# Attention and tree layers on one core: scores and the next maxima back to back on eight shared PSUM banks, and the product with v once per group

## The chip, the cores and the metric

The kernel runs on one core of a Trainium2 chip. The time is the device time of one execution in microseconds, over 3 runs. Its core has TensorE (PE; PEld are its weight loads), VectorE (DVE), ScalarE (ACT), GpSimd (POOL) and SyncE (SP, which issues all DMAs here).

## The reference

Eight sequences of 512 tokens with 256 features pass through four residual layers. All is float32.

```python
x = x + attn_a(layernorm(x))    # 16 heads of 16, biases, softmax over all 512 keys
x = x + ffn(layernorm(x))       # below
x = x + attn_b(layernorm(x))    # 16 heads of 16, rotary q and k, causal softmax
x = x + ffn(layernorm(x))       # the same ffn, the same weights

def ffn(x):
    gate = sigmoid((x @ Wq.T) @ routers.T)       # 255 nodes of a binary tree, depth 8
    leaf_prob = product over the 8 levels of (1 - gate) or gate     # 256 leaves
    return (leaf_prob @ leaf_values) @ Wout.T + Wout_b
```

An attention layer computes `softmax(q k^T / 4) v` for each of the 16 heads, and then a product with an output matrix.

## The kernel before

**Sequences, groups, steps.** The program handles 16 "sequences" n: n = 0 to 7 are the eight batch rows in the first attention and tree layer (non-causal), n = 8 to 15 the same rows in the second (causal). A sequence has four groups g of four heads (NG = NJ = 4), and a group has four tiles of 128 keys, kt. One group and one kt make a step: 16 steps a sequence, 256 in all.

**Scores.** q and k are split into a high and a low part and laid out so that one head takes 32 partitions. Four heads then use four row groups of TensorE at a time, as 32*128 matmuls (`passes`, L416). `scores` computes transposed scores st[keys, queries] for one kt into four PSUM banks: two matmuls per head with k against the two arrangements of q, and a third (`ones` against `m`) that subtracts each query's maximum. ScalarE then writes exp of it to the SBUF tiles pt (L481). In the causal half, st has only the queries from kt * 128 on, and GpSimd clears the upper triangle of the diagonal block (L484).

**Maxima.** The row maxima are found earlier from untransposed scores mx (`maxima`, two matmuls per head, four banks). VectorE reduces each bank to one column (L444; with the mask in the causal half, L439). After four tiles of queries, VectorE makes `less` (L448, L449), TensorE transposes it (`lessT`, in `put`), ScalarE copies it to `rows` (L460), and a DMA puts it into one of two tiles m (L461). The maxima run LEAD = 12 half-steps, that is six steps, ahead of the scores.

**Product with v.** `weigh` multiplies v with pt as 128*32 matmuls (L498), one head per column group, right after the scores of the next step. It adds the four kt of a group up in a bank of its own (`ps_av`), so av has one bank and seven banks rotate among all other tiles (`bank`, pool `banks`). Every fourth kt ScalarE copies av to o4 (L504), and DMAs carry sums and outputs on to `divide`.

**Everything else** is cut into units, generators that a small planner (`Units`) advances: `pre` (LayerNorm, transposes, q, k and v of a coming sequence), `post` and `tree` (output product y, LayerNorm, gates z, the tree's levels lp on VectorE, transposes lt, leaf values ty), `divide`, `put`. Each unit names its kind ("big" and "small" for TensorE, "v" VectorE, "g" GpSimd, "row") and a delay. In each step `share` grants TensorE a budget of TENSOR = 11 and VectorE one of 3900, and `products` pulls units until TensorE's is used up. Full-width products and transposes use the whole array (128*128). The row x of each sequence stays in SBUF from its load at the start to the store at the end: eight tiles x0 to x7.

**Order.** The loop runs over half-steps i. An even i issues the maxima of the step six steps ahead and then products; an odd i issues the scores of this step, then `weigh` of the step before. `in_program_order` ties each engine's instructions to the order in which the program issued them, so an engine never overtakes, and a DMA that waits on SP holds those behind it.

Of the kernel before, what the change touches and what calls it, by code (L numbers as in the profile page):

```python
# [41 lines left out]
F32 = mybir.dt.float32  # L42
# [20 lines left out]
STEPS = NG * NT * 2  # L63
LEAD = 12

EARLY = 6


FULL, TRANSPOSE, TENSOR = 12, 4, 11
# [7 lines left out]
class Units:  # L77
# [40 lines left out]
    def share(self):  # L118
        self.tensor = min(self.tensor, TENSOR // 2) + TENSOR
        self.vector = min(self.vector, VECTOR // 2) + VECTOR  # L120
# [19 lines left out]
def hybrid_kernel(ctx, tc, x, a_qk, a_v, a_o, a_qk_b, a_v_b, a_o_b, b_q, b_k, b_v, b_o,  # L140
# [3 lines left out]
    stream = ctx.enter_context(tc.tile_pool(name="stream", bufs=1))  # L144
# [18 lines left out]
    xs = []  # L163

    def load_x(b):
        t = stream.tile([P, NT, D], F32, tag=f"x{b}", name=f"x{b}")
        nc.sync.dma_start(t, x[b].rearrange("(t p) d -> p t d", p=P))
        xs.append(t)
# [8 lines left out]
    for m in ms:  # L177
# [19 lines left out]
    pool5 = ctx.enter_context(tc.tile_pool(name="w5", bufs=5))  # L197
# [3 lines left out]
        for w, n, tag in ((f_q, "f_q", "lpT"), (f_routers, "f_routers", "th"),  # L201
                          (f_values, "f_values", "lp"), (f_out, "f_out", "out"))
    ]
    banks = ctx.enter_context(tc.tile_pool(name="banks", bufs=7, space=PSUM))
    dram = ctx.enter_context(tc.tile_pool(name="apart", bufs=2, space=bass.MemoryType.DRAM))
    ps_av = ctx.enter_context(tc.tile_pool(name="ps_av", bufs=1, space=PSUM))
# [7 lines left out]
    for b in range(3, B):  # L214
        load_x(b)
# [4 lines left out]
    vs, ks, qs, outs, avs, lesses = [], {}, {}, {}, {}, {}  # L220
# [28 lines left out]
    def fold_bias():  # L249

        vb = pool1.tile([P, NC, P], F32, tag="vb", name="vb")
        for c in range(NC):
            nc.vector.tensor_copy(vb[:, c, :], v_b[:, c : c + 1].to_broadcast([P, P]))
        ps = bank([P, D], "vbo")
        for c in range(NC):
            nc.tensor.matmul(ps, lhsT=vb[:, c, :], rhs=wa.o[:, c, :], start=c == 0, stop=c == NC - 1)
        nc.vector.tensor_tensor(out_b, ps, out_b, ALU.add)

    def layer_norm(b, name, got):

        x = xs[b]
        stats = pool2.tile([P, NT, 6], F32, tag="ln_stats", name=f"ln_stats{name}")
        mv = pool2.tile([P, NT, 2], F32, tag="ln_mv", name=f"ln_mv{name}")
        for t in range(NT):
            nc.vector.bn_stats(stats[:, t, :], x[:, t, :])
            nc.vector.bn_aggr(mv[:, t, :], stats[:, t, :])
            units.spend(vector=D + 2 * START)
            if t == 1:
                yield "v", 0
        yield "g", 1  # L270
        less_mean = pool2.tile([P, NT], F32, tag="ln_less", name=f"ln_less{name}")
        nc.gpsimd.tensor_scalar(less_mean, mv[:, :, 0], -1.0, None, ALU.mult)
        rstd = pool2.tile([P, NT], F32, tag="ln_rstd", name=f"ln_rstd{name}")
        nc.gpsimd.tensor_scalar(rstd, mv[:, :, 1], EPS, None, ALU.add)
        nc.gpsimd.tensor_tensor(rstd, rstd, neg_half, ALU.pow)
        xn = pool2.tile([P, NT, D], F32, tag="xn", name=f"xn{name}")
        for t in range(NT):
            if t % 2 == 0:
                yield "g", 0
            nc.gpsimd.tensor_scalar(  # L280
                xn[:, t, :], x[:, t, :], less_mean[:, t : t + 1], rstd[:, t : t + 1], ALU.add, ALU.mult
            )
        got.append(xn)

    def add_bias(b, bias):
        for t in range(0, NT, 2):
            yield "g", 0
            part = xs[b][:, t : t + 2, :]
            nc.gpsimd.tensor_tensor(part, part, bias.unsqueeze(1).to_broadcast([P, 2, D]), ALU.add)
# [50 lines left out]
    def pre(n):  # L340

        causal, b = divmod(n, B)
# [6 lines left out]
        w = wb if causal else wa  # L349
        got = []  # L350
        yield from layer_norm(b, f"n{n}", got)
# [14 lines left out]
        free = (n - 1) * STEPS + 2 + LEAD  # L366
        vals[n] = units.add(by_tokens(xnT, w.v, D, f"v{n}", values), "big", max(1, free - units.now), rank=4)
        for which in range(2):
# [3 lines left out]
            for c in range(NC):  # L372
                yield "big", 0 if c or which else 1
# [34 lines left out]
        if not causal:  # L408
            yield from add_bias(b, out_b)
# [8 lines left out]
    def maxima(n, g, u):  # L418

        causal = n >= B  # L420
        qt = (u + LEAD // 2) % NT
# [43 lines left out]
    def scores(n, g, kt):  # L465
# [12 lines left out]
        for pair in range(2):  # L478
            pt = pool5.tile([P, 2, S], F32, tag="pt", name=f"pt{n}_{g}_{kt}_{pair}")
# [11 lines left out]
    def weigh(n, g, kt, pts):  # L491

        if kt == 0:
            avs[n, g] = ps_av.tile([P, S], F32, tag="av", name=f"av{n}_{g}")
        av = avs[n, g]
        first = kt * P if n >= B else 0
        for j in range(NJ):
            nc.tensor.matmul(  # L498
                av[32 * j : 32 * j + 32, first:], lhsT=vs[n % 2][:, kt, g * NJ + j, :, :].rearrange("p d s -> p (d s)"),
                rhs=pts[j // 2][:, j % 2, : S - first], start=kt == 0, stop=kt == NT - 1,  # L500
            )
        if kt == NT - 1:
            o4 = pool1.tile([P, S], F32, tag="o4", name=f"o4{n}_{g}")
            nc.scalar.copy(o4, avs.pop((n, g)))  # L504
            if g == 0:
                outs[n] = (
                    pool2.tile([P, NC, S], F32, tag="out", name=f"out{n}"),
                    pool2.tile([P, NC, S // HD], F32, tag="few", name=f"few{n}"),
                )
            outT, few = outs[n]  # L510
            to, c = slice(g % 2 * 64, g % 2 * 64 + 64), g // 2
            nc.sync.dma_start(few[to, c, :], o4[1 :: 2 * HD, :])
            nc.sync.dma_start(outT[to, c, :], o4[::2, :])
            if g % 2:
                units.add(divide(n, c), "v", 3, rank=0)
# [19 lines left out]
    def to_x(b):  # L535
        def add(ps, t, count):
            part = xs[b][:, t : t + count, :]
# [5 lines left out]
    def post(n):  # L543

        causal, b = divmod(n, B)
# [3 lines left out]
        yield from by_tokens(outT, (wb if causal else wa).o, D, f"y{n}", to_x(b))  # L549
        yield "v", 1  # L550
        yield from tree(n, b)

    def tree(n, b):
# [4 lines left out]
        yield from layer_norm(b, f"t{n}", got)  # L558
# [15 lines left out]
        yield from add_bias(b, f_bias)  # L574
# [23 lines left out]
        yield from by_tokens(lpT, wl, D, f"ty{n}", to_x(b), 1)  # L598
        if n >= B:
            nc.sync.dma_start(out[b].rearrange("(t p) d -> p t d", p=P), xs[b])  # L600
# [14 lines left out]
    waiting = deque()  # L615
    for i in range(-LEAD, total + 2):
# [5 lines left out]
        for n in range(2, 2 * B):  # L622
            if ahead == (n - 1) * STEPS - (EARLY if n >= B else 0):
                if n >= B:
                    units.finish(trees[n - B])
                pres[n] = units.add(pre(n), rank=1 if n >= B else 3)
        if i % STEPS == 0 and i // STEPS in vals:
            units.finish(vals.pop(i // STEPS))
        if i % 2 == 0:
            units.share()  # L630
            if ahead < total:
                maxima(*place(ahead))
            units.products()
        else:
            if 0 <= i < total:
                waiting.append((*place(i), scores(*place(i))))
            if len(waiting) > 1 or (i >= total and waiting):
                weigh(*waiting.popleft())
            units.pull("row")
# [76 lines left out]
```

## Time and profile before

| | |
|---|---|
| median of 3 runs (lowest, highest) | 1237.98 us (1235.34, 1238.89) |
| profiled execution | 1241.78 us, its span 1240.1 us |
| busy in the span | PE 1157.4, PEld 602.2, DVE 854.0, ACT 639.0, POOL 412.2 us |
| mean granted clock of TensorE | 0.944 |
| DMA queue q1 | 81.55 MB, 18.6% of 16 engines |

The span runs from the first to the last instruction. Busy times of different engines overlap. The ends of matmuls are modelled, so that PE's busy time holds some waits too; the starts are what can be compared. The chain of waits is followed back from the last instruction to what released each step. A group's idle time is that of its engine just before it, with the instruction that ended it.

### The profile page before, as it was taken

To read this page: it belongs to the slowest core of one execution; us is meant where nothing else is said; L and a number is where in the kernel's file an instruction comes from. 1 tells how busy PE (TensorE), PEld (TensorE's weight loads), DVE (VectorE), ACT (ScalarE), POOL (GpSimd) and SP (SyncE) were. 2 spreads that over 40 slices of the span, in tenths; PEclk is the share of its full clock that TensorE was granted. 3 is DMA by queue.
4 is the path that set the end of the run, shared out by engine and by line. 5 is a ranking of instruction groups with operands and counts; after the bars stand their busy time and mean duration, and the time that the engine had idled before them with its cause. 6 is when DMAs were issued, how large, how long until landed. Compare 5 with 4: busy or idle time off the path is not lost.

```text
span 1240.1 us, 24920 instructions
## 1 busy us (share of the span) xinstructions
PE 1157.4 (93%) x8916; PEld 602.2 (49%) x8916; DVE 854.0 (69%) x2400; ACT 639.0 (52%) x1457; POOL 412.2 (33%) x636
## 2 busy tenths in 40 slices
PE   4899999999999999999999989999999999999965
PEld 2444444545445354444455555555545455555443
DVE  2766686776777578778878786867778686767422
ACT  2266566575666557655564534545353544534431
POOL 3222232230323213322244444444443445423331
PEclk9699999999999899999999999989898998988788
DMA  8031103021030301303030211213021211310110
GB/s 314 18 113 67 71 19 118 19 84 49 16 122 20 115 13 41 121 20 121 16 121 13 89 62 44 94 37 121 26 87 53 86 70 37 122 33 21 37 36 17
DMA packets 61211, 83.14 MB, mean 67 GB/s; under 512 B 14752, under 2 KB 27808, under 8 KB 61088
## 3 DMA queue, kind: packets, MB, share of 16 engines
q1 hardware_dynamic: 61088, 81.55, 18.6%
q8 instruction: 70, 1.15, 0.4%
q14 instruction: 53, 0.43, 0.1%
HBM read 16.52 MB, written 4.72 MB: 17 GB/s over the span
## 4 chain that ended last, share of the span: by engine, by line
PE 69%; DVE 16%; DMA 4%; POOL 4%; issue 4%; ACT 3%; SPq 1%; DVEq 0%; ACTq 0%; POOLq 0%
PE st L416 16%; PE av L498 13%; PE mx L416 11%; PE qk L376 7%; DVE seen L439 6%; PE ty L310 6%; PE v L310 5%; PE z L310 5%; PE y L310 3%; DVE most L444 3%; ACT pt L481 2%; DVE lp L589 2%; POOL xnt L280 2%; DMA m<-rows 1%; DMA q<-hl 1%
## 5 line engine op out<-in xcount | busy, mean ns | idle before, releaser
L481 ACT ACTIVATE pt<-st 128x512 f32<-128x512 f32 (+3 forms) x1024 | 446.8, 523 | 334.3 <-PE st L416 332.5
L444 DVE TENSOR_REDUCE most<-mx 128x1 f32<-128x512 f32 x512 | 317.2, 682 | 163.6 <-PE mx L416 163.4
L439 DVE CUSTOM_DVE_ANT_0 seen<-mx,mask 128x128 f32<-128x128 f32 (+3 forms) x512 | 250.6, 490 | 129.4 <-PE mx L416 72.5
L416 PE MATMUL st<-q,k 32*128 32x512 f32 (+3 forms) x2048 | 240.5, 426 | 22.4 <-DVE most L439 15.0
L498 PE MATMUL av<-pt,v 128*32 128x512 f32 (+3 forms) x2048 | 238.2, 537 | 3.5 <-POOL pt L484 2.3
L416 PE MATMUL mx<-k,q 32*128 32x512 f32 (+3 forms) x2048 | 210.1, 427 | 16.8 <-DMA k<-hl 5.8
L484 POOL TENSOR_SCALAR_AFFINE_SELECT pt<-pt 128x256 f32<-128x256 f32 x256 | 110.5, 440 | 318.7 <-ACT pt L481 315.8
L416 PEld LDWEIGHTS st<-q,k 32*128 32x128 f32 x2048 | 114.5, 187 | 152.6 <-issue 66.4
L416 PEld LDWEIGHTS mx<-k,q 32*128 32x128 f32 x2048 | 102.3, 192 | 169.4 <-issue 36.0
L416 PE MATMUL st<-m,ones 32*128 32x512 f32 (+3 forms) x1024 | 118.5, 365 | 1.3 <-DMA m<-rows 1.3
L322 POOL TENSOR_TENSOR hl<-r,hl 128x512 fp32r<-128x512 f32 x32 | 41.7, 1304 | 190.5 <-ACT hl L392 184.5
L310 PE MATMUL ty<-wl,lpT 128*128 128x256 f32 x256 | 80.4, 471 | 0.0
L498 PEld LDWEIGHTS av<-pt,v 128*32 128x32 f32 x2048 | 41.1, 109 | 78.7 <-issue 59.2
L416 PEld LDWEIGHTS st<-m,ones 32*128 32x128 f32 x1024 | 70.7, 190 | 9.3 <-DMA m<-rows 3.4
L589 DVE SCALAR_TENSOR_TENSOR lp<-th,lp 128x8 f32<-128x8 f32 (+6 forms) x224 | 70.2, 353 | 2.9
L310 PE MATMUL z<-wg,txnT 128*128 128x255 f32 x256 | 68.5, 408 | 0.0
L310 PEld LDWEIGHTS ty<-wl,lpT 128*128 128x128 f32 x256 | 57.4, 235 | 18.0 <-ACT pt L481 5.5
L376 PE MATMUL qk<-xnT,a_qk 128*128 128x512 f32 x128 | 63.9, 635 | 0.0
L376 PE MATMUL qk<-xnT,b_qk 128*128 128x512 f32 x128 | 62.9, 617 | 0.0
L310 PEld LDWEIGHTS z<-wg,txnT 128*128 128x128 f32 x256 | 47.7, 199 | 17.1 <-ACT pt L481 7.1
L531 POOL TENSOR_TENSOR out<-out,den 128x512 f32<-128x512 f32 x32 | 41.4, 1294 | 35.8 <-DMA den<-apart 35.6
L396 POOL TENSOR_TENSOR r<-r,r 128x512 f32<-128x512 f32 x32 | 40.3, 1278 | 24.8 <-DVE r L387 24.8
(76 smaller groups left out, 1101.4 us busy)
## 6 DMA issues: line engine op xcount, KB each, us to landing
q<-hl SPq DMA_DIRECT2D x128, 256.0 KB
k<-hl SPq DMA_DIRECT2D x64, 256.0 KB
out<-o SPq DMA_DIRECT2D x64, 128.0 KB
den<-apart SPq DMA_DIRECT2D x32, 256.0 KB
x<-x SPq DMA_DIRECT2D x8, 512.0 KB
out<-x SPq DMA_DIRECT2D x8, 512.0 KB
m<-rows SPq DMA_DIRECT2D x64, 16.0 KB
few<-o SPq DMA_DIRECT2D x64, 8.0 KB
```

The lines of the kernel that those rows point to most:

```text
L310: nc.tensor.matmul(ps[:, i, :n], lhsT=srcT[:, c, (t + i) * P : (t + i + 1) * P], rhs=w[:, c, :], start=c == 0, stop=c == NC - 1,)
L322: on.tensor_tensor(hl[:, 1, :], raw, hl[:, 0, :].bitcast(F32), ALU.subtract)
L376: nc.tensor.matmul(ps, lhsT=wt[:, k, c * P : (c + 1) * P], rhs=xnT[:, k, :], start=k == 0, stop=k == NC - 1,)
L396: nc.gpsimd.tensor_tensor(raws[c], raws[c], raws[2 + c], (ALU.subtract, ALU.add)[c])
L416: nc.tensor.matmul(ps, lhsT=lhsT, rhs=rhs, start=i == 0, stop=i == len(operands) - 1)
L439: nc.vector.tensor_tensor_reduce(out=seen[:, :width], in0=ps[:, :width], in1=mask[:, S - width :], scale=1.0, scalar=LOWEST, op0=ALU.add, ...
L444: nc.vector.tensor_reduce(at, ps, AX.X, ALU.max)
L481: nc.scalar.activation(pt[:, i, : S - first], ps[:, : S - first], AF.Exp, scale=SCALE)
L484: nc.gpsimd.affine_select(out=pt[:, :, :P], in_=pt[:, :, :P], pattern=[[0, 2], [1, P]], compare_op=ALU.is_ge, fill=0.0, base=0, channel_mu ...
L498: nc.tensor.matmul(av[32 * j : 32 * j + 32, first:], lhsT=vs[n % 2][:, kt, g * NJ + j, :, :].rearrange("p d s -> p (d s)"), rhs=pts[j // 2 ...
L531: nc.gpsimd.tensor_tensor(outT[:, c, :], outT[:, c, :], den, ALU.mult)
L589: nc.vector.scalar_tensor_tensor(pairs[:, :, :, side], of_level, one, lp, ALU.add, ALU.mult)
```

## The change

The odd and even half-steps are merged: one turn of the loop issues the scores of a step and, directly behind them, the maxima of the step six steps ahead. The bank for av is given up, and eight banks rotate among all tiles. `weigh` is called once per group, after the first step of the next group, with all four kt (16 products); for that, ten pt tiles are kept where there were five. Products follow at the end of a turn; TENSOR is 15, and a call of `weigh` costs WEIGH = 13 of it. The order of query tiles in `maxima` becomes 1, 2, 3, 0. `pre` of a coming sequence starts EARLY = 8 half-steps earlier in both halves, has rank 2, and holds its q and k products back until 24 half-steps into the sequence two back.

To make room in SBUF, only AT_ONCE = 5 tiles x exist. The tree of each sequence of the first half stores its row to DRAM (`store_x`), and `pre` of a later sequence loads what it needs (`load_x`), three half-steps before LayerNorm reads it. Three scratch tiles share the buffers of others, and the scratch ring of GpSimd's DMAs is set to 8192.

```diff
-EARLY = 6
-FULL, TRANSPOSE, TENSOR = 12, 4, 11
+AT_ONCE = 5
+EARLY = 8
+FULL, TRANSPOSE, WEIGH, TENSOR = 12, 4, 13, 15
...
-        self.tensor = min(self.tensor, TENSOR // 2) + TENSOR
+        self.tensor = min(self.tensor, TENSOR // 4) + TENSOR
...
+    def load_x(n):
+        t = stream.tile([P, NT, D], F32, tag="x", name=f"x{n}")
+        src = x[n] if n < B else between[n - B]
+        nc.sync.dma_start(t, src.rearrange("(t p) d -> p t d", p=P))
+        xs[n] = t
+
+    def store_x(n):
+        dst = between[n] if n < B else out[n - B]
+        nc.sync.dma_start(dst.rearrange("(t p) d -> p t d", p=P), xs.pop(n))
...
-    pool5 = ctx.enter_context(tc.tile_pool(name="w5", bufs=5))
+    pool10 = ctx.enter_context(tc.tile_pool(name="w10", bufs=10))
...
-    banks = ctx.enter_context(tc.tile_pool(name="banks", bufs=7, space=PSUM))
+    banks = ctx.enter_context(tc.tile_pool(name="banks", bufs=8, space=PSUM))
...
-    ps_av = ctx.enter_context(tc.tile_pool(name="ps_av", bufs=1, space=PSUM))
...
+        if n not in xs:
+            units.finish(trees[n - AT_ONCE])
+            load_x(n)
+            yield "v", 3
...
-                yield "big", 0 if c or which else 1
+                free = (n - 2) * STEPS + 24 + LEAD
+                yield "big", 0 if c or which else max(1, free - units.now)
...
-        qt = (u + LEAD // 2) % NT
+        qt = (1, 2, 3, 0)[u]
...
-    def weigh(n, g, kt, pts):
-        if kt == 0:
-            avs[n, g] = ps_av.tile([P, S], F32, tag="av", name=f"av{n}_{g}")
-        av = avs[n, g]
+    def weigh(n, g, group):
+        av = bank([P, S], f"av{n}_{g}")
+        for kt, pts in enumerate(group):
...
-        if n >= B:
-            nc.sync.dma_start(out[b].rearrange("(t p) d -> p t d", p=P), xs[b])
+        store_x(n)
...
-        if i % 2 == 0:
-            units.share()
-            if ahead < total:
-                maxima(*place(ahead))
-            units.products()
-        else:
-            if 0 <= i < total:
-                waiting.append((*place(i), scores(*place(i))))
-            if len(waiting) > 1 or (i >= total and waiting):
-                weigh(*waiting.popleft())
-            units.pull("row")
+        units.share()
+        full = group if len(group) == NT else None
+        if full:
+            group = []
+        if 0 <= i < total:
+            group.append(scores(*place(i)))
+        if ahead < total:
+            maxima(*place(ahead))
+        units.reductions()
+        units.pull("g")
+        units.tick()
+        if full:
+            weigh(*place(i - 2)[:2], full)
+            units.spend(tensor=WEIGH)
+        units.pull("row")
+        units.products()
```

## The prediction

> **What bounds the kernel now.** I read the page first, then the waits, the timeline of one step, and the windows around a stretch of low clock.
>
> ```profile
> span 1240.1 us, 24920 instructions
> PE 1157.4 (93%) x8916; PEld 602.2 (49%) x8916; DVE 854.0 (69%) x2400; ACT 639.0 (52%) x1457; POOL 412.2 (33%) x636
> ...
> PE 69%; DVE 16%; DMA 4%; POOL 4%; issue 4%; ACT 3%; SPq 1%; DVEq 0%; ACTq 0%; POOLq 0%
> ```
>
> TensorE carries 69% of the chain that ended last, VectorE 16%. Nothing else matters, so the question is what fills TensorE's 93%. One step (a kt of one group) without causal mask reads:
>
> ```profile
> 303.51 0.74 PE L416 MATMUL mx<-k,q 32*128 32x512 f32 x8
> 304.18 1.99 PE L310 MATMUL y<-a_o,out 128*128 128x256 f32 x8
> 306.10 0.74 PE L416 MATMUL st<-q,k 32*128 32x512 f32 x8
> 306.66 0.41 PE L416 MATMUL st<-m,ones 32*128 32x512 f32 x4
> 307.01 1.06 PE L498 MATMUL av<-pt,v 128*32 128x512 f32 x8
> 308.00 0.74 PE L416 MATMUL mx<-k,q 32*128 32x512 f32 x8
> 308.57 0.39 PE L416 MATMUL st<-q,k 32*128 32x512 f32 x1
> ```
>
> Take differences of starts, not durations. Inside a block the single records of the trace start one pass (four matmuls side by side in four row groups, 512 columns) every 0.216 us. So mx is worth 0.432, but takes 0.67 (303.51 to 304.18); y is worth 8 x 0.216 = 1.73 and takes 1.92; st with ones 0.648 and takes 0.91. About 0.21 us goes at every change between the shapes 32*128, 128*32 and 128*128, but 0.13 into 128*32. The step has four such changes, **0.76 us of 4.49**.
>
> At 308.57 there is no product between mx and st, and st stops after one matmul. The waits say why:
>
> ```profile
> PEld st L416 <- DVE most L439: 29.0, 58, 1.7
> PEld st L416 <- DVE most L444: 12.7, 40, 1.4
> ```
>
> With seven banks in rotation, st of such a step gets the banks of the mx just issued, and VectorE needs 2.4 us (4 x 0.60) to reduce those. In the causal half a third loss appears (columns: window, then busy us of PE, PEld, DVE, ACT, POOL, then granted clock):
>
> ```profile
> 803.20:806.70 3.50, 2.50 (x32) 1.55 (x31) 3.03 (x12) 1.37 (x5) 0.63 (x2) 0.99 0.00 0
> 806.70:810.10 3.40, 3.19 (x16) 1.82 (x15) 2.83 (x16) 0.59 (x1) 1.65 (x4) 0.50 0.00 0
> ```
>
> Each causal sequence has one stretch of about 10.2 us at half clock, after a window in which TensorE streamed only some 30% of the time (matmul records at one column a cycle).
>
> **The Trainium skill.** "TensorEngine Tiling (Array Packing)", Key Properties: changing the tiling mode drains TensorE. The trace agrees: 0.11 us on the way out and 0.10 on the way in. "PSUM — Partial Sum Buffer", Specifications: eight banks per partition, so the change uses all of them. "TensorE: Matmul & The Clock Gate", Part 1: activity is judged in windows of 3.413 us, and an idle one halves the clock. The trace agrees on the grid (half-clock stretches last 3.41, 6.83 or 10.24 us), but here windows that streamed up to 0.42 already trigger, and it took 0.76 or more to recover.
>
> **The change, part by part.** The sum is against the profiled execution: 1241.8 us in all, span 1240.1; the median is 1238.0, 3.8 lower.
>
> (1) *Mode changes.* In the order of the built programs, TensorE changes shape family 956 times before and 573 after: into 128*32 from 257 times to 128, into 32*128 from 475 to 235, into 128*128 from 224 to 210 (before, lessT rides along with av and is counted in 128*32). 129 x 0.13 + 240 x 0.21 + 14 x 0.21 = **70 us less work on TensorE**. Not all of it reaches the end, since VectorE gets no less.
>
> (2) *Who is the longer one in each step.* I count each step's TensorE work (passes and changes as above; av 0.866 per kt, a 256-column product 0.432, a transposed tile 0.12) and VectorE's (non-causal maximum 0.60; causal 0.44, 0.58, 0.71, 0.84 by width, start to start; bn_stats 0.43; 0.07 plus 1.04 ns per column for the others), in the order of the built program. After, sequence 5, TensorE/VectorE, in us: 5.96/2.40, 3.23/3.18, 4.33/3.14, 3.23/3.48, 5.96/3.61, 2.45/2.70, 4.33/3.34, 4.10/4.39, 4.89/3.45, 3.23/3.30, 2.33/3.71, 1.29/3.45, 6.61/2.40, 3.23/2.70, 2.33/2.40, 4.09/2.40. The larger ones sum to 66.1 (before 68.5). After, causal sequence 11: 4.66/3.97, 2.75/3.75, 3.79/4.24, 2.64/3.91, 4.66/4.57, 1.96/3.27, 3.79/3.24, 3.50/4.83, 3.59/4.42, 2.75/2.67, 1.79/3.61, 0.70/3.89, 5.31/4.57, 2.75/3.27, 1.79/2.30, 3.49/3.43: 62.2 (before 65.2), of which VectorE alone is 59.9. Over sequences 0 to 7 the sums are 542 before and 523 after, over 8 to 14 454 and 432. **So 42 of the 70 us arrive; VectorE keeps the rest.** The same sums for before, held against its trace (585 and 495 us for these sequences), leave 43 and 41 us above them: half clock about 5 and 36, waits about 42.
>
> (3) *Bank turn-round, a new wait.* With scores and maxima back to back, eight banks are full when the block ends, and what follows (product, lessT or av) takes the bank of st's first tile. ScalarE's first exp starts 0.49 after the first ones pass (306.66, 307.15) and takes 0.60, so the bank is free 0.56 + 0.49 + 0.60 + 0.06 = 1.71 us after the block starts; TensorE arrives at 1.32. That is 0.39 in each step in which TensorE is the longer: ten per non-causal and four per causal sequence, 8 x 10 + 7 x 4 = 108 steps, **+42 us**; after q/k products, where ScalarE first spends 1.16 on r and hl, some 0.26 more, 4 x 8 x 0.26 = 8. From below it is 0 (VectorE's lag hides it); from above 1.0 a step, if ScalarE is behind by one more tile. What it replaces are the 42 us of waits in (2). Steps also overlap by about a step where VectorE lags, worth 0.8 a sequence, -12. A VectorE-bound step with no other VectorE work (sequence 11's fifteenth) sees a bubble of about 0.8 between its last reduction and the next tile; two a causal sequence, +11. Net of the old waits: 42 + 8 - 12 + 11 - 42 = **+7**.
>
> (4) *Half clock.* In the twelfth step TensorE has 1.29 (0.70 causal) against VectorE's 3.5 to 3.9, so a window below 0.42 is likely there, but the next step is av plus q/k products, dense for 5 us or more, which restores the clock after one or two windows (a loss of 1.7 to 3.4) instead of three (5.1). Causal 7 x -2.5 = -17; non-causal, where it is new, 8 x +0.5 = +4. Net **-13**, bounds -36 and +20.
>
> (5) *x in DRAM.* Eleven later loads and eight stores of 512 KB between the halves. out<-x landed 2.8 us after its issue; LayerNorm reads x three half-steps after the load is queued, and the first load of the next sequence stands one step behind av, so about 3 us are left: cost 0, at most 2 us for each of 11 if SP is late. SP is also held by the store until VectorE has added ty (before, eight such waits, longest 34.6 us); behind it stands only o4's transport to division, 6 half-steps away.
>
> (6) *SP's queue in the non-causal half.* For sequences 2, 4, 5, 6 and 7 four q DMAs, which wait for st of the sequence two back, now stand ahead of m<-rows of the next sequence's first group. They issue every 0.65; m follows at 0.55 + 2.6 and lands 1.8 (to 3.3 behind traffic) later, 4.95 to 6.4 us after that st; ones wants it at 5.0. **+3**, bounds 0 and 10. Nothing hides it but the z products of that step.
>
> (7) *Ten pt tiles*: av runs a group later, so the POOL select (0.44 each, with 1.28 us adds ahead of it) no longer delays av. The 8.5 us of "POOL pt" ahead of av go; they are in the waits of (3). What is late instead is the last group's av, four kt in one: +2 in the tail.
>
> Sum: -42 + 7 - 13 + 3 + 2 = -43: 1199 in the profiled execution, 1195 in the median; I say **1197**.
>
> **The rivals.** (a) *As above*, 1180 to 1218. For it: the count of changes is exact and VectorE's load is known. (b) *More arrives*: two thirds of the 50 us of turn-round in (3) hide in VectorE's lag: 1195 - 33, about 1162. For it: VectorE lags in half of the steps. Against it: every step ends in a full set of banks. (c) *VectorE binds*: it has 50 to 60 us of a 62 to 66 us sequence, and an in-order wait of 0.4 us in half of the steps (8 x 15 x 0.4) adds 48, less the 11 in (3): 1195 + 37, about 1232. For it: 59.9 of 62.2. (d) **Slower**: ScalarE's turn-round. If the wait for the first bank is not 0.39 but more than 0.8 us in the 108 steps, 108 x 0.41 = 44 us more are gone and nothing is left; at 1.0, one exp late, 108 x 0.61 = 66: 1195 + 66 = 1261. For it: ScalarE gets its copies of products in the same queue ahead of the exps; against: it is busy 52%. (e) That mode changes don't fall is excluded by the order; that TensorE stops inside the block instead is (c).
>
> **How the numbers follow.** Chances: (a) 0.50, (b) 0.20, (c) 0.15, (d) 0.15. About 0.3% (3.7 us) is what can be told from no change; a third of (c) lies within it: faster 0.80, same 0.05, slower 0.15. The range takes (a), most of (b) and (c): 1160 to 1236.
>
> **What would show it.** Right: st and mx blocks follow each other 0.22 apart without a gap; PE av has 64 blocks of 32; "PEld st <- DVE most" shrinks, and a wait of TensorE (y, v, qk, av) for ACT pt of some 0.4 us appears in most steps; DVE busy about 854 in a shorter span, 71%; half-clock stretches in the causal half get shorter than 10 us. Wrong: ACT pt waits near 1 us (d), mx waiting for DVE in most steps (c), or ones waiting for DMA m beyond 10 us.

## The result, and the profile after

The changed kernel takes **1326.7 us** (median of 4 runs, 1321.4 to 1331.2). Against the kernel before (1237.3 us beside it) that is a ratio of **1.072, interval 1.068 to 1.077**: 7% slower, 130 us above the forecast and outside its range. The profiled execution has a span of 1326.2 us. Its page answers to the first fence of the prediction:

```profile
span 1326.2 us, 24827 instructions
PE 1128.9 (85%) x8916; PEld 627.2 (47%) x8916; DVE 867.4 (65%) x2397; ACT 643.6 (49%) x1460; POOL 405.1 (31%) x636
...
PE 54%; DVE 18%; DMA 10%; ACT 6%; issue 5%; POOL 4%; SPq 1%; DVEq 0%; ACTq 0%; POOLq 0%
...
L431 PE MATMUL st<-m,ones 32*128 32x512 f32 (+3 forms) x1024 | 108.9, 392 | 68.0 <-DMA m<-rows 67.9
```

TensorE falls from 93% to 85% of a longer span, and its mean granted clock from 0.944 to 0.916, so the loss is idle time and clock, not work. The chain that ended last names a newcomer: DMA, from 4% to 10%. The last line says where: ahead of the third pass of the scores, which adds the row of maxima with `ones`, TensorE idled 68 us for the transfer m<-rows. The waits show the same, and the smaller ones that step (3) of the prediction spoke of (columns: us in total, times, longest):

```profile
PEld st L431 <- DMA m<-rows: 83.6, 34, 6.7
PE st L431 <- DMA m<-rows: 67.9, 29, 6.2
PEld st L431 <- ACT pt L496: 38.1, 96, 0.8
...
PEld mx L431 <- DVE r L402: 29.9, 24, 1.7
...
PE mx L431 <- DVE r L402: 24.2, 24, 1.4
```

In the kernel before there was next to none of this:

```profile
PEld st L416 <- DMA m<-rows: 3.4, 5, 1.0
```

The step itself, where m is not late, looks as forecast:

```profile
403.38 0.74 PE L431 MATMUL st<-q,k 32*128 32x512 f32 x8
403.96 0.40 PE L431 MATMUL st<-m,ones 32*128 32x512 f32 x4
404.19 0.63 PE L431 MATMUL mx<-k,q 32*128 32x512 f32 x8
405.10 1.13 PE L319 MATMUL ty<-wl,lpT 128*128 128x256 f32 x4 [0.28 <-ACT pt L496]
```

The three blocks follow each other without a gap. The product that comes next starts 1.72 us after the block (405.10 less 403.38); the prediction had the bank of the first exponential free after 1.71.

Why m is late is seen in the queue of SP. First the kernel before, at the end of an odd group, from the timeline of all engines:

```profile
379.93 0.41 DVE L449 SCALAR_TENSOR_TENSOR less<-most,less 128x16 fp32r<-128x16 f32 x1
...
384.33 0.34 DVE L524 RECIPROCAL inv<-few 128x32 f32<-128x32 f32 x1
384.69 0.32 SPq L527 DMA_DIRECT2D apart<-inv  x1
...
386.11 0.62 SPq L529 DMA_DIRECT2D den<-apart  x1
386.13 0.25 ACT L460 COPY rows<-lessT 32x128 f32<-32x128 f32 x1
386.82 0.62 SPq L461 DMA_DIRECT2D m<-rows  x1
```

And the changed kernel, at the same place of the sequence:

```profile
417.35 0.17 DVE L464 SCALAR_TENSOR_TENSOR less<-most,less 128x16 fp32r<-128x16 f32 x1
...
419.71 0.25 ACT L475 COPY rows<-lessT 32x128 f32<-32x128 f32 x1
...
421.19 0.34 DVE L537 RECIPROCAL inv<-few 128x32 f32<-128x32 f32 x1
...
421.56 0.33 SPq L540 DMA_DIRECT2D apart<-inv  x1
...
423.05 0.60 SPq L542 DMA_DIRECT2D den<-apart  x1
...
423.75 0.62 SPq L476 DMA_DIRECT2D m<-rows  x1
...
427.39 0.80 PE L431 MATMUL st<-m,ones 32*128 32x512 f32 x4 [3.48 <-DMA m<-rows]
```

In both, m stands behind the two transfers of `divide` on SP: apart<-inv waits for the reciprocal, and den<-apart waits until apart has landed. Before, the reciprocal came 1.8 us ahead of the copy of the rows, and m could be issued 0.44 us after that copy. After, it comes 1.5 us behind the copy. It is the copy that has moved: counted from the end of `less`, the rows are ready after 6.4 us before and after 2.3 us now, while the reciprocal starts after 4.4 and 3.6 us (medians of the odd groups). So the rows, ready at 419.96, wait for SP until 423.75. m lands 3.6 us later, behind den's 256 KB (1.8 us is what it takes alone), and `ones` starts 0.04 us after that. By the start of `ones` against the landing, 34 of 64 groups wait like this, against 5 before: 30 odd groups, and the first groups of sequences 3 to 6, where m stands behind q transfers and `ones` waits only 0.5 us.

For all that, m does not land later than it did: in the odd groups it lands 10.6 us after `less` before and 9.7 us after it now (medians). What has become shorter is the time until it is wanted. `ones` came 12.6 us after `less` before; in run 1 below, where nothing of the division stands ahead of m, it comes after 5.0 us. The turns between the two no longer hold a product with v and are short: the scores that follow `less` start at 420.01 and 421.71 here, and at 383.15, 387.92 and 391.52 before.

### The profile page after: what moved, and what is told of

Its sections match the earlier page's. It is cut to its first block, busy times and chain, and to the rows that moved or that the text cites. A ratio compares the mean times of both kernels' runs of the same rounds, so it can differ in the third digit from the quotient of the medians.

```text
span 1326.2 us, 24827 instructions
## 1 busy us (share of the span) xinstructions
PE 1128.9 (85%) x8916; PEld 627.2 (47%) x8916; DVE 867.4 (65%) x2397; ACT 643.6 (49%) x1460; POOL 405.1 (31%) x636
## 4 chain that ended last, share of the span: by engine, by line
PE 54%; DVE 18%; DMA 10%; ACT 6%; issue 5%; POOL 4%; SPq 1%; DVEq 0%; ACTq 0%; POOLq 0%
PE av L512 16%; PE st L431 10%; DMA m<-rows 8%; PE mx L431 7%; PE qk L391 6%; DVE seen L454 6%; ACT pt L496 4%; PE z L319 4%; DVE most L459 4%; PE ty L319 3%; PE v L319 3%; DVE r L402 2%; PE y L319 2%; DVE less L464 2%; DMA apart<-inv 1%
## 5 line engine op out<-in xcount | busy, mean ns | idle before, releaser
L454 DVE CUSTOM_DVE_ANT_0 seen<-mx,mask 128x512 f32<-128x512 f32 (+3 forms) x512 | 250.7, 490 | 141.2 <-PE mx L431 84.2
L431 PE MATMUL mx<-k,q 32*128 32x512 f32 (+3 forms) x2048 | 237.5, 410 | 50.5 <-DVE r L402 24.2
L431 PE MATMUL st<-q,k 32*128 32x512 f32 (+3 forms) x2048 | 206.9, 414 | 4.2 <-ACT v L376 2.3
L431 PEld LDWEIGHTS mx<-k,q 32*128 32x128 f32 x2048 | 137.5, 197 | 109.7 <-DVE r L402 29.9
L431 PE MATMUL st<-m,ones 32*128 32x512 f32 (+3 forms) x1024 | 108.9, 392 | 68.0 <-DMA m<-rows 67.9
L431 PEld LDWEIGHTS st<-q,k 32*128 32x128 f32 x2048 | 96.9, 186 | 118.4 <-issue 54.5
L512 PEld LDWEIGHTS av<-pt,v 128*32 128x32 f32 x2048 | 69.9, 125 | 167.8 <-issue 122.2
L517 ACT COPY o<-av 128x512 f32<-128x512 f32 x64 | 37.5, 587 | 148.4 <-issue 135.8
L431 PEld LDWEIGHTS st<-m,ones 32*128 32x128 f32 x1024 | 57.2, 193 | 88.4 <-DMA m<-rows 83.6
L319 PE MATMUL ty<-wl,lpT 128*128 128x256 f32 x256 | 65.3, 401 | 2.3 <-ACT pt L496 1.8
```

The costliest lines, as they stand in the source:

```text
L319: nc.tensor.matmul(ps[:, i, :n], lhsT=srcT[:, c, (t + i) * P : (t + i + 1) * P], rhs=w[:, c, :], start=c == 0, stop=c == NC - 1,)
L431: nc.tensor.matmul(ps, lhsT=lhsT, rhs=rhs, start=i == 0, stop=i == len(operands) - 1)
L454: nc.vector.tensor_tensor_reduce(out=seen[:, :width], in0=ps[:, :width], in1=mask[:, S - width :], scale=1.0, scalar=LOWEST, op0=ALU.add, ...
L512: nc.tensor.matmul(av[32 * j : 32 * j + 32, first:], lhsT=vs[n % 2][:, kt, g * NJ + j, :, :].rearrange("p d s -> p (d s)"), rhs=pts[j // 2 ...
L517: nc.scalar.copy(o4, av)
```

## The experiments

All ratios are to the kernel before, measured beside each run.

**1. m ahead of the division on SP.** One number: the division is due one half-step later, so its two transfers queue behind m.

```
-            units.add(divide(n, c), "v", 3, rank=0)
+            units.add(divide(n, c), "v", 4, rank=0)
```

> The changed kernel with the unit of divide due one half-step later, so that on SP the DMA m<-rows of an odd group stands ahead of apart and den instead of behind them. Theory S (SP's order makes the maxima late): the 32 odd groups lose their 2 to 3 us each that ones waits for m, the five groups behind q DMAs keep theirs, and some half clock goes with it: 1230 to 1260 us. Rival T (the turn-round of the eight banks at the first exp costs the 90 us): hardly anything, 1305 or more. Rival X (traffic of x through DRAM): nothing, 1320 to 1330.

Measured: 1260.1 us, ratio 1.015 (1.011 to 1.019), 67 us below the changed kernel and at the upper end of what theory S gave. Groups whose `ones` waits for m fall from 34 to 5, and the waits of TensorE for m are no longer among the large ones:

```profile
PEld st L431 <- ACT pt L496: 39.7, 103, 0.8
...
PEld mx L431 <- DVE r L402: 33.6, 29, 1.7
...
PEld av L512 <- ACT pt L496: 28.2, 48, 1.1
...
PEld st L431 <- DMA m<-rows: 2.6, 5, 0.8
```

So the place of m in SP's queue is worth 67 us (the half clock that goes with it included), and 20 us of the loss against the kernel before remain.

**2. The same by another way: m issued from ScalarE's queue.**

```
-        nc.sync.dma_start(ms[g % 2].bitcast(F32)[:: HD, :], rows)
+        nc.scalar.dma_start(ms[g % 2].bitcast(F32)[:: HD, :], rows)
```

> The changed kernel with m<-rows issued from ScalarE's own queue right after its copy to rows; apart, den and the q DMAs can't hold it. Theory S: no wait of TensorE for m above 5 us in all; faster than the one with the later divide by some 10 us (the groups behind q DMAs), less up to 0.6 us of ScalarE for each of 64 issues: 1215 to 1250 us. T: 1305 or more. X: 1320 to 1330.

Measured: 1262.8 us, ratio 1.018 (1.015 to 1.021), and no wait for m at all. It agrees with run 1. The 10 us more that the expectation gave to the q transfers of step (6), which this way also gets past, did not come: in run 1 four groups wait 0.5 us each behind them.

**3. x through DRAM alone, in the kernel before.**

```
-    stream = ctx.enter_context(tc.tile_pool(name="stream", bufs=1))
+    stream = ctx.enter_context(tc.tile_pool(name="stream", bufs=AT_ONCE))
...
+        if n not in xs:
+            units.finish(trees[n - AT_ONCE])
+            load_x(n)
+            yield "v", 3
...
+        store_x(n)
```

> The kernel before with nothing but the five x tiles: rows are stored to DRAM after their first tree and loaded again ahead of LayerNorm. Theory S: the store holds SP until VectorE has added ty, but m has 1 to 5 us in hand there: within 10 us of before, 1230 to 1250. Rival X: 1280 or more.

Measured: 1258.6 us, ratio 1.012 (1.007 to 1.017), between the two theories. The prediction had this part at 0. It lies in the causal sequences: 0 to 7 take 582 us together (587 before), 8 to 14 take 525 (494 before). Much of it goes with the half clock, 173 us in place of 142: of its four executions three took 1258.5 to 1259.6 us at a mean granted clock of 0.929 to 0.932, and one, at 0.948, took 1246.4.

**4. The transfers of run 3 without its order.** All eight x stay in SBUF, the store to DRAM and a second transfer of the copy, inside DRAM, are added on SP, and nothing waits for them.

```
+            nc.sync.dma_start(spare[b].rearrange("(t p) d -> p t d", p=P), between[b].rearrange("(t p) d -> p t d", p=P))
...
+        dst = out[b] if n >= B else between[b]
+        nc.sync.dma_start(dst.rearrange("(t p) d -> p t d", p=P), xs[b])
```

> The kernel before with all eight x in SBUF and its order of work unchanged, but with the transfers of the changed kernel added on SP's queue: x of the first eight sequences is stored to DRAM after the tree, and where the next layer begins the stored copy is moved once more inside DRAM, which nothing waits for. Theory T (traffic and queue): the 15 to 20 us that x through DRAM cost came from the transfers, which hold SP and the DMA queues in front of the maxima's and the divide's: 1248 to 1260 us. Rival P (the planner): they came from the three half-steps that the load yields and the shifted order of the products in sequences 8 to 14: within 5 us of the kernel before.

Measured: 1243.1 us, ratio 1.005 (1.003 to 1.006), nearer to rival P; its half clock is 145 us. A third of run 3's cost is the transfers; two thirds come with the loads into shared tiles, the half-steps they yield and the half clock that follows, which the two runs do not separate.

**5. The load of x taken out of the planner's order, on top of run 1.** The next x is loaded by the tree that has freed the tile.

```
         store_x(n)
+        if n + AT_ONCE < 2 * B:
+            yield "v", 6
+            load_x(n + AT_ONCE)
```

> The kernel with the maxima's transfer first (1260.1 us), and the next x of its tile loaded six half-steps after the tree has stored the old one, instead of in front of the next layer norm; the three half-steps that this load put into the planner's order go. The added transfers alone cost the kernel before 6 us, x through DRAM as a whole 15 to 20, so most of that cost should be the order of the work that the yielded half-steps shift. Theory P (order): 1243 to 1253 us. Rival: the order of the changed kernel is another one, in which these three half-steps shift nothing that TensorE waits for: 1257 to 1264 us.

Measured: 1270.8 us, ratio 1.028 (1.021 to 1.034), 11 us slower than run 1. The theory fell: what the loads do to the order is not a cost that comes off when they are moved. Sequences 3 to 5 stay near 73 us, the causal ones go from about 71.7 to as much as 75.4. The half clock is 182 us in both kernels, so it is not the reason; the reason is open.

**6. The products between scores and maxima, on top of run 1.**

```
-        if ahead < total:
-            maxima(*place(ahead))
         units.reductions()
...
         units.products()
+        if ahead < total:
+            maxima(*place(ahead))
```

> This is the kernel with the maxima's transfer ahead of the divide's, with one thing more: in each turn the product and the other products now stand between the scores and the maxima on TensorE, and not behind the maxima. Theory B (banks): in the order scores, maxima, products the next turn's maxima want the bank of a product that was written just before, and the product wants the bank of this turn's first exponential. The profile of that kernel shows TensorE waiting in the maxima for r 26 us, for hl 7 us and for x 10 us, and about 100 turns lose 0.37 us ahead of a product. With a product between, four scores and the product are further apart from the banks that they reuse: the waits of the maxima for r, hl and x fall below 10 us in all and the time to 1195 to 1225 us. Rival O (the uneven steps): the first turn of a group carries the product of four key tiles and two projections, its length of 9 to 11 us beside turns of 1.4 to 1.7 us is what costs, and the order inside a turn does little: 1250 to 1270 us. Rival V: VectorE gets its maxima later in the turn, idles first, and then holds the next turn: above 1270 us.

Measured: 1430.2 us, ratio 1.157 (1.153 to 1.160); of the theories only V allows that much. The banks of the exponentials no longer hold anything up (TensorE's weight loads wait 2 us for pt, 131 in run 1), but something else does, and the half clock rises from 182 to 377 us, which is at most 97 of the 170 us:

```profile
PEld lessT L473 <- DVE less L464: 140.9, 64, 4.7
PE lessT L473 <- DVE less L464: 118.9, 64, 4.0
...
PE lt L304 <- DVE lp L602: 38.7, 13, 4.8
```

The transposition of the maxima now stands right behind the maxima in TensorE's order, with VectorE's reduction between them, 1.9 us in each of 64 groups. With m moved to ScalarE's queue as well the order gave 1442.5 us:

> The products between scores and maxima, the maxima's transfer ahead of the divide's, and that transfer issued by ScalarE instead of SP, so that the q transfers cannot stand ahead of it either. Theory B: the maxima end later in a turn here, their path to the row of ones is some 1 to 2 us shorter in slack, and freeing it from SP's queue gives 0 to 8 us against the same kernel with SP: 1190 to 1225 us. If it is 10 us or more slower than with SP, ScalarE's own instructions are delayed by the wait of that transfer for its row copy. Rival O: within 8 us of 1260 us.

So m was not what held it; TensorE's waits for m are under 2 us in the first of the two runs.

**7. The same order with those two waits taken away.** lessT goes behind the products, the leaves' transposition is due two half-steps later.

```
-        units.pull("row")
         units.products()
+        units.pull("row")
...
-            yield "small", 0 if c else 1
+            yield "small", 0 if c else 3
             transposed(lpT, lp, c, f"lt{n}_{c}")
```

> The products between scores and maxima once more, with the two waits taken away that this order brought: the transposition of the maxima (lessT) now stands behind the turn's products and not ahead of them, and the leaves' transposition (lt) is due two half-steps later. In the run with the products between, TensorE waited 119 us in lessT for less and 39 us in lt for lp, while its waits for the exponentials' banks had fallen from 131 to 2 us (weight loads). Theory B (banks cost the most of what is open): without the two waits 1430 us falls by about 158 us and by the half clock that they brought, to 1195 to 1250 us. Rival V (VectorE): the maxima reach VectorE last in each turn, it idles in long turns and holds TensorE in short ones (the waits for most rose from 34 to 122 us in that run and stay there), so what the banks give is lost again: 1255 to 1300 us.

Measured: 1292.7 us, ratio 1.042 (1.037 to 1.047). The time is the one that rival V gave: waits for pt are 5 us, waits for most 161 us (34 in run 1; weight loads, all rows summed). The waits of lessT did not go altogether: 26 us of matmul waits for less are left of 119. So what the order gave at pt came back at most.

**8. The product once per group alone, in the old order of the turn.** Run 3's kernel, with ten tiles of exponentials, its seven shared banks and its own bank for av.

```
-                waiting.append((*place(i), scores(*place(i))))
-            if len(waiting) > 1 or (i >= total and waiting):
-                weigh(*waiting.popleft())
+                waiting.append(scores(*place(i)))
+            if len(waiting) > NT or (i >= total and waiting):
+                weigh(*place(i - 2)[:2], [waiting.popleft() for _ in range(NT)])
+                units.spend(tensor=WEIGH)
```

> One part alone: the kernel before with x of five sequences through DRAM (which alone ran at 1258.6 us), and the product with v once per group from ten tiles of exponentials. Scores and maxima stay in alternate half-turns with the products between, the seven shared banks and the bank for av stay, and the planner has the changed kernel's budget of products. Theory M (the saving of mode changes arrives, and the order back to back is what loses it again in the changed kernel): some 380 fewer mode changes give 50 to 70 us, 1190 to 1215 us. Rival S (the product of each key tile was also the space in which the exponentials and maxima freed their banks; without it TensorE waits there in any order): 1235 to 1275 us, with TensorE's waits for most and pt well above the 87 and 89 us of the kernel before. If the maxima's transfer is late here too, ones waits for m above 20 us, and the time is above 1275 us.

Measured: 1363.3 us, ratio 1.101 (1.095 to 1.108), 105 us slower than run 3 with fewer mode changes (629 in place of 955 in the order of the traces). Neither theory had that much. Rival S gives the direction, but only half of its sign came: waits for most rise from 91 to 133 us, those for pt fall from 102 to 82 (weight loads). TensorE waited only 2 us for m there, and 84 us more than in run 3 were at half clock (257 against 173), which is 42 us of time at most; the planner's budget differs too, so the 105 us are not one cause. The timeline of TensorE shows what the product of each key tile had covered:

```profile
556.31 0.73 PE L428 MATMUL st<-q,k 32*128 32x512 f32 x8
556.88 0.40 PE L428 MATMUL st<-m,ones 32*128 32x512 f32 x4
557.21 0.28 PE L470 MATMUL lessT<-ident,less 128*32 128x128 f32 x1
557.43 1.81 PE L428 MATMUL mx<-k,q 32*128 32x512 f32 x8
559.17 1.99 PE L318 MATMUL v<-a_v,xnT 128*128 128x256 f32 x8
```

The maxima take 1.81 us for eight matmuls that take 0.74 where nothing holds them. They come right behind the scores, and wait head by head for banks that have not been read yet (here the weight loads wait for pt, ScalarE's exponentials; over the run those of the maxima wait 69 us for most and 40 for pt). Before, av stood in that place in every turn.

How much such waiting there is in each kernel is seen best from block starts: the mean time from the first matmul of a block to the first of the next block, in us, worked out from the trace (av per key tile; first figure us 68 to 640 of the span, second 640 to 1160; roughly the sequences without and with the causal mask, though in the slower kernels the second stretch begins up to 77 us ahead of the mask). It takes in every wait inside the block and of the block that follows, and the half clock.

| block | before | after | run 1 | run 8 |
|---|---|---|---|---|
| mx | 0.73 / 0.77 | 1.08 / 1.20 | 1.07 / 1.29 | 1.38 / 1.13 |
| st, two passes | 0.72 / 0.79 | 1.02 / 0.78 | 0.72 / 0.50 | 0.81 / 0.70 |
| ones | 0.41 / 0.34 | 0.26 / 0.21 | 0.22 / 0.23 | 0.33 / 0.33 |
| av | 1.00 / 0.70 | 1.05 / 0.78 | 0.97 / 0.71 | 0.95 / 0.63 |
| sum | 2.86 / 2.60 | 3.41 / 2.97 | 2.98 / 2.73 | 3.47 / 2.79 |

In run 1 the saving is there in `ones` (0.41 to 0.22) and in the causal st (0.79 to 0.50); the maxima give it back, 0.34 and 0.52.

**9. The bank of a projection read by one instruction, on top of run 1.** The maxima of the next turn waited for banks that held q and k products.

```
-                        nc.vector.tensor_tensor(raws[-1], ps, table, ALU.mult)
+                        nc.vector.tensor_tensor(raws[-1], raw, table, ALU.mult)
...
+                    raw = pool1.tile([P, S], F32, tag="raw", name=f"raw{n}{which}{c}")
+                    nc.scalar.copy(raw, ps)
...
-                    for to in (raws[c], hls[c][:, 0, :]):
-                        nc.scalar.activation(to, ps, AF.Identity, bias=w.qk_b[:, at : at + 1])
+                    nc.scalar.activation(raws[c], ps, AF.Identity, bias=w.qk_b[:, at : at + 1])
+                    nc.scalar.copy(hls[c][:, 0, :], raws[c])
```

> The kernel with the maxima's transfer first, and the bank of a q or k projection read by one instruction instead of two: in the causal layers ScalarE copies it to SBUF and VectorE makes both products with cos and sin from the copy, in the others hl is copied from r in SBUF. Theory B (a projection right ahead of the next turn's scores and maxima holds a bank that the maxima want): TensorE's waits in the maxima for r and hl, 51 us for weight loads and 33 us for matmuls, fall below a third; 1232 to 1248 us. Rival W: the four maxima wait for VectorE's and ScalarE's next instruction instead (most, pt), and the sum stays: 1254 to 1265 us.

Measured: 1252.1 us, ratio 1.007 (1.003 to 1.011), between the two theories. The waits for r and hl, 84 us in weight loads and matmuls, fall below 3, with 8 for `raw`, which now reads the bank; the time falls by 8. The waits for pt and most rise (131 to 149 us and 34 to 48, weight loads), among them:

```profile
PEld st L433 <- ACT pt L498: 44.9, 109, 0.9
...
PEld av L514 <- ACT pt L498: 27.3, 49, 1.1
PEld lessT L475 <- ACT pt L498: 24.7, 41, 2.3
PEld qk L391 <- ACT pt L498: 20.2, 36, 0.9
```

Together with run 5's load the bank gave 1266.7 us, ratio 1.021 (1.018 to 1.025), 15 us slower than the bank alone; here too the load by the tree costs:

> Both at once: x loaded by the tree, and the projections' banks read by one instruction. If theories P and B both hold, 1220 to 1240 us, which is level with or below the kernel before; if neither does, 1255 to 1265 us; if the product once per group takes away the cover in which banks come free, what is gained at one wait is lost at the next and the time stays above 1245 us.

**10. The half clock.** At this point the trace had 182 us at half clock in run 1 and 189 in run 9, against 142 before and 224 after. Run 9's kernel gets matmuls that nothing reads, ahead of the causal scores of key tiles 2 and 3:

```
+        if n >= B and kt >= 2:
+            for j, ps in enumerate(got):
+                rows = slice(32 * j, 32 * j + 32)
+                for q in qs[n]:
+                    nc.tensor.matmul(ps, lhsT=ks[n][rows, g, kt * P : (kt + 1) * P], rhs=q[rows, g, :], start=True, stop=True)
         passes(todo)
```

> The kernel with the maxima's transfer first and the projections' banks read by one instruction (1252.1 us), with matmuls added that nothing reads: in the causal layers the scores of key tiles 2 and 3 are preceded by eight matmuls of 512 columns into the same banks, which the scores then overwrite. They add 0.86 us of streaming to each of 64 turns in which TensorE has little to stream. Theory H (the half clock): sequences 10 to 13 lose 10 to 14 us each at half clock after a stretch in which TensorE streams a quarter of the time; filled, that falls below 4 us, and as the added 0.86 us lies beside VectorE's maxima, the time falls by 10 to 30 us to 1222 to 1242 us. Rival T (TensorE is the bound in these turns too): the clock rises, but 64 times 0.86 us come on top: 1260 to 1300 us.

Measured: 1243.1 us, ratio 1.004 (1.002 to 1.005): 9 us faster with 37 us of matmuls added. (The expectation's 0.86 us per turn is too much: from the first added matmul to the first of the scores the trace shows 0.57 us, and 64 x 0.57 is 37.) Half clock falls from 189 to 127 us; sequences 11 to 13 go from 70.0, 71.4 and 71.4 us to 68.3 each. The windows show one causal stretch, first run 9, then this one (us of busy PE, PEld, DVE, ACT, POOL, then the granted clock, DMA share, GB/s):

```profile
956.00:1028.00 72.00, 66.94 (x576) 39.86 (x568) 55.02 (x188) 36.38 (x94) 31.74 (x54) 0.91 0.22 76
```

```profile
956.00:1028.00 72.00, 67.10 (x654) 41.83 (x652) 57.52 (x198) 36.51 (x97) 32.89 (x56) 0.98 0.25 86
```

VectorE gets 4.5% more of its work done in the same 72 us. The same matmuls in the kernel before:

> The kernel before with the same matmuls added, for the dose of the half clock there: its causal sequences show 10.2 us of half clock each, after a stretch at 0.30 of streaming around the scores of key tile 3. Theory H: that half clock goes, 5 us a sequence at most, and 1237 us becomes 1205 to 1230 us. Rival T: the added 55 us of streaming fall on the path in part, 1245 to 1285 us.

Measured: 1244.0 us, ratio 1.004 (1.002 to 1.006), half clock 98 us in place of 142. Theory H was wrong for this kernel: 44 us less at half clock are worth 22 us at most, and the added matmuls cost what that was worth and 6 more.

**11. A weight of the causal layers loaded earlier, and half of the filling.** The load of b_o goes to its own tile at the change of layers, and to make room for it the scratch ring of GpSimd's DMAs goes from 8192 to 4096; what the ring does by itself was not run. In the second run the added matmuls stand ahead of key tile 3 alone.

```
+            wb.o = load(b_o, "b_o", tag="b_o")
...
-        if n == B:
-            wb.o = load(b_o, "b_o", tag="w_o")
```

```
-        if n >= B and kt >= 2:
+        if n >= B and kt == 3:
```

> The kernel of the filled run in the changed kernel's family (1243.1 us), and the causal layers' output weight loaded into a tile of its own at the change of layers, not behind the last use of the other layers' weight. In that family's profiles sequence 9 takes 80 to 82 us where the kernel before takes 72: TensorE waits there 3 us for the weight and 4.3 us for k<-hl behind it, and 20 us of the sequence run at half clock. If those two transfers make it, sequence 9 falls to 70 to 75 us and the time to 1230 to 1237 us, below the kernel before; rival: k<-hl is late for another reason, sequence 9 stays above 78 us and the time at 1240 to 1245 us.

> The same with the added matmuls ahead of key tile 3 alone, half of them. If the half clock is set off by the stretch around key tile 3 alone, it stays away and half of the added 55 us of streaming is saved where TensorE is the later engine: 1222 to 1234 us. Rival: one filled turn is too little, the half clock returns to 10 us or more in sequences 10 to 13, and the time is 1236 to 1248 us.

Measured: 1239.8 us, ratio 1.001 (0.999 to 1.003), and **1233.2 us, ratio 0.996 (0.995 to 0.997)**. Sequence 9 fell from 81.6 to 76.7 us and not to 75: the wait for k<-hl there stayed at 4 us, so b_o was only part of it. With half of the filling the half clock stays away (0 to 3.4 us in sequences 10 to 13, each 66.8 to 67.8 us). The last run is 0.4% below the kernel before, the only version of the change that is. The kernel before was not run with half of the filling or with the earlier load, so it is not shown that the gain is the change's.

## Why the prediction was wrong, by its steps

**(6), SP's queue, is the step that failed**: +3, bounds 0 and 10; runs 1 and 2 measured 67 and 64 us. What it did look at it had nearly right: the q transfers ahead of m make four groups wait, 2 us in all. It put at nothing the transfers that stood ahead of m already, the division's of every odd group. They had been harmless because `ones` came 12.6 us after `less` (median of the odd groups). Now it wants m after 5.0 us. The rows are ready in time for that, as lessT follows `less` within 1.3 us (5.1 before); but the reciprocal, which had come before the copy of the rows, comes behind it, m still lands only after 9.7 us, and 30 of 32 odd groups wait. The order of SP's list was read for what the change added to it, not for what stood there. The line under "Wrong", ones waiting for m beyond 10 us, was the right place to look.

**(1)** and the block of (3) hold: the traces have 956 and 573 mode changes, scores and maxima run without a gap, `ones` falls from 0.41 to 0.22 us from start to start, and the bank turn-round is 1.72 us in the block shown, where 1.71 was forecast.

**(3), the sum, was mis-sized.** The old waits left as forecast (VectorE's most in weight loads, 86 to 34 us in run 1), but those that came were larger. The wait for the first exponential was given to ten non-causal turns of sixteen (the turns listed for sequence 5 have nine in which TensorE is the longer, those for sequence 11 six and not four; that changes 2 us). It came in all: in the 91 non-causal turns of run 1 that can be read whole at full clock, no next block starts before 1.6 us after the scores, where 1.32 would be without a wait. 48 start at 1.6 to 1.8, 31 at 1.8 to 2.1 (most of these behind q and k products, for which the step has 1.97), and the mean is 1.95. If the other turns are alike, that is 128 x 0.63 = 81 us where the step has 31 and 8; in turns in which VectorE is the longer one, part of it is hidden. The mean also holds what the step leaves out, that the maxima themselves wait for the banks of the q and k products: run 1 shows 33 us of matmul waits for r and hl in the whole program. Run 8 points to what the step lacked: av of each key tile had been the cover, and in three of four turns the change takes it away. Runs 6 and 9 took single waits away, 129 us for pt and 84 us for r and hl; the first made the kernel slower, and of the second 8 us arrived.

**(4), the half clock, had the wrong sign.** -13 was forecast; the changed kernel has 82 us more at half clock than the kernel before, run 1 has 40 more, which is at most 20 us of time. The shorter stretches did come in the changed kernel: causal sequences 10 to 13 show 6.8, 6.8, 10.2 and 6.8 us in place of 10.2 each. In run 1 they are at 10.2 again. (Before, there is also a stretch of 27.3 us at the start and one of 13.7 near the end.) What grew lies elsewhere, in run 1 in sequences 0 to 2, 7 and 9, with 6 to 21 us more in each; the step had +0.5 us of time for a non-causal sequence. Part of the 67 us of run 1 is this too: its half clock is 42 us below the changed kernel's.

**(5), x in DRAM at 0**: 18 us in the kernel before (run 3; 8 to 21 by its interval), about 6 of them transfers (run 4). In the changed kernel the share is not known, since moving the load made it slower (run 5).

**(7)** is not told apart, as no run changed it. The last sequence with the tail takes 109 us in both kernels, and av's waits for GpSimd's pt, which were to go, are 9.7 us (8.5 before).

The rivals: (d) gave the sign. Its mechanism is there in part: the wait behind the maxima, up to 0.63 us in the mean of those turns, lies between the 0.39 of (a) and the more than 0.8 that (d) asks for. Half of the 130 us between forecast and result came from m, which no rival had. What stays open: of the 63 us between run 1 and the forecast, the bank turn-round can be up to 42 us, the half clock 33 (-13 forecast, +20 at most found) and x in DRAM 18. These overlap, and the runs do not split them further, as single waits hand over to the next.

## What to carry to other kernels

When an edit moves a result closer to its use, or changes which of two short chains is ready first, read the queue that both pass: a 16 KB transfer behind one that waits cost 67 us, and one number put it right. Work that looks like an overhead of TensorE (a product per tile, a mode change) may be the cover in which other engines empty banks; before it is bunched, name what stands between a bank's writer and its next user in the turns that lose it. A wait taken away is worth its sum only if the next wait behind it is named too.

## What was not expected of the hardware

A transfer of 16 KB landed 1.8 us after its issue alone, and 2.9 to 3.8 us after it in the 30 groups of the changed kernel where it was issued right behind one of 256 KB on the same queue. Matmuls whose result nobody reads can pay: in run 10 37 us of them (64 turns of 0.57 us) went with 9 us less time, as half clock fell from 189 to 127 us. In run 11 half as many, with a weight loaded earlier (worth 3 us before the halving), went with 19 us less than run 9, at 131 us of half clock. In the kernel before, the 64 turns cost 6 us.
